# Nine products for twelve: sharing the q convolution's differences in both directions

## The chip, the cores and the metric

The kernel runs on one core of a Trainium2 chip. The metric is the device time of one execution in microseconds; lower is better. One execution of the kernel was also recorded by the profiler, and all views below come from that one.

## The reference

The input is a batch of 8 images with 256 channels of 64 x 64. Two layers follow each other. Layer 0 is an attention whose keys and values come from a 4 x 4 strided convolution of the image; its result is added to the image. Layer 1 is a linear attention at two scales:

```
qkv = einsum('oc,bchw->bohw', w_qkv, x)                # 768 channels
dw  = conv(qkv, w_dw, 5x5, padding 2, one filter per channel)
agg = einsum('goi,bgihw->bgohw', w_pw, dw in groups of 8)
ms  = concatenate([qkv, agg])                          # 64 heads, each 8 channels of q, k and v
q, k = relu(q), relu(k);  kv = k^T [v, 1];  out = q kv[:-1] / (q kv[-1] + 1e-15)
return x + batchnorm(w_proj out)
```

The change concerns the branch `agg`, and in it the q third: the depthwise 5 x 5 filter and the mixing of 8 channels into 8, together one convolution of 8 channels by 8 in each of 32 groups, followed by relu.

## The kernel before

The work goes in three passes over the batch, all in float32.

The **first pass** does layer 0 and the product with `w_qkv`, and writes q and k to HBM as *planes*: an image is cut into 16 phases (position within 4 x 4 cells), the 128 partitions hold 16 phases of a group of 8 channels, and the free dimension holds the cells, 17 x 17 with their border. On the side the generator `conv_weights` multiplies the depthwise and the mixing weights into the convolution's matrices and writes them to HBM (`wtd[j]`; j of 0 and 1 is q, 2 and 3 is k). A step of it runs once per step of the main loop, from step 17 on.

The **second pass** (`second_pass`) goes over 64 units `(t, k, b)`: half, block of four groups, image; the image runs fastest, so weights serve eight units. For a unit it convolves k (`what = 1`), forms the sums over positions of k with v at both scales (`summed_raw`, `summed`), and convolves q two units later (`what = 0`, for `q = u - 2`). A product maps the 128 values of a group's cell (16 phases by 8 channels) to the 128 values of an output cell; an output cell needs four of them, from the 2 x 2 input cells around it, so a square of 2 x 2 output cells would take 16. The kernel before shares products across only: for each pair of columns, `paired` (L1189 and L1190) makes the differences d0 - d1 and d2 - d1, and `convolve` computes three products instead of four, each for two rows `da` that are summed in PSUM, which makes 12 per square. A product with 128 columns covers a unit's 16 rows by 8 pairs of columns, so there are 3 x 2 x 4 groups = 24 of them per unit and convolution, recorded as 48 matmuls, since a float32 product appears as two records; L1248 issues those of k, L1252 those of q. The part with `i == 2` is common to both columns: ScalarE copies it from PSUM to the tile `both` (L1255), VectorE adds it to the other two (L1264), and ScalarE rectifies the sums into `r` (L1266 for k, L1268 for q).

All DMAs are issued by queue SP, in one order. For a unit these are: the tokens `kq` and `vq` of the next unit (L1165, L1177), the cells `d` of k and of q (L1158), the previous results `kv` and `kvg` (L1330, L1340), four stores of `r` to `qd` (L1347), and one of the four pieces of the next block's weights (L1152). Each of q's and k's weights has two buffers, used by turns, and so have the q cells. The framework places instructions on each queue by its own estimate, roughly in the order of the program, except for those marked `keep_in_program_order`.

The **third pass** divides and projects. Its first loads and products are called from the last units of the second (`next(ahead)`).

Of the kernel before, what the change touches and what calls it, by code (L numbers as in the profile page):

```python
# [27 lines left out]
F32 = mybir.dt.float32  # L28
# [546 lines left out]
def first_pass(ctx: ExitStack, tc: tile.TileContext, a, fine, planes, x2d, kd, vd, wtd):  # L575
# [98 lines left out]
    def conv_weights():  # L674
        for j in (2, 3, 0, 1):
            wd = made.tile([P, 16, 6, 16], F32, tag="wd", name=f"wd_{j}", bufs=1)
            nc.sync.dma_start(wd[:, :, :4], a.w_big[:, j].rearrange("p g (n f) -> p g n f", n=4))

            tc.keep_in_program_order(nc.vector.tensor_add(wd[:, :, 4:], wd[:, :, 0:4:2], wd[:, :, 1:4:2]))
            for g in range(16):  # L680
                w = made.tile([P, 6 * 16, D1], F32, tag="wb", name=f"wb_{j}_{g}", bufs=1)
                tc.keep_in_program_order(
                    nc.vector.tensor_tensor(
                        w,
                        wd[:, g].rearrange("p n f -> p (n f)").unsqueeze(2).to_broadcast([P, 6 * 16, D1]),
                        consts["wsmall"][:, j, g].unsqueeze(1).to_broadcast([P, 6 * 16, D1]),
                        ALU.mult,
                    )
                )
                nc.sync.dma_start(wtd[j][:, g], w.rearrange("p n o -> p (n o)"))  # L690
                yield
# [427 lines left out]

@with_exitstack  # L1120
def second_pass(ctx: ExitStack, tc: tile.TileContext, a, planes, kd, vd, wtd, kvd, kvg, qd, ahead):
    nc = tc.nc
    B = a.x.shape[0]
    def pool(name, bufs=1):
        return ctx.enter_context(tc.tile_pool(name=name, bufs=bufs))
# [3 lines left out]
    late, first, odd, const, second, small, mid, w_taps, pairs, sides, between, third, third_w, w_q, more = (  # L1129
        pool("late2", 2), pool("first2"), pool("odd2"), pool("const2"), pool("second2"), pool("small2", 2),  # L1130
        pool("mid2"), pool("taps2"), pool("pairs2", 2), pool("sides2", 2), pool("between2", 2), pool("third2"),
        pool("third_w2"), pool("wq2"), pool("more2"),
# [11 lines left out]
    wt, grids, cells, kqs, vqs = {}, {}, {}, {}, {}  # L1144


    def load_weights(u, what, g):
        t, k, b = units[u]
        if g == 0:
            home = (second if k % 2 else first) if what else (third_w if k % 2 else w_q)  # L1150
            wt[t, k, what] = home.tile([P, 4, 6 * P], F32, tag=f"w{what}_{k % 2}", name=f"w{what}_{t}_{k}")
        nc.sync.dma_start(wt[t, k, what][:, g], wtd[2 * what + t][:, 4 * k + g])  # L1152

    def load_cells(u, what):
        t, k, b = units[u]
        home = (odd if u % 2 else first) if what else (more if u % 2 else third)
        d = home.tile([P, 4, (NB + 1) ** 2], F32, tag=f"d{what}_{u % 2}", name=f"d{what}_{u}")
        nc.sync.dma_start(d, planes[b, 2 * what + t][4 * k : 4 * k + 4].rearrange("g p e -> p g e"))  # L1158
        grids[u, what] = d.rearrange("p g (y x) -> p g y x", x=NB + 1)
# [24 lines left out]
    def paired(u, what):  # L1184
        d = grids[u, what]
        c = (pairs if what else late).tile([P, 2 + what, 4, (NB + 1) * NB // 2], F32, tag=f"c{what}", name=f"c{what}_{u}")
        v = c.rearrange("p n g (y x) -> p n g y x", x=NB // 2)
        d0, d1, d2 = (d[:, :, :, i : i + NB - 1 : 2] for i in range(3))
        nc.vector.tensor_sub(v[:, 0], d0, d1)  # L1189
        nc.vector.tensor_sub(v[:, 1], d2, d1)  # L1190
        if what:

            nc.gpsimd.tensor_copy(v[:, 2], d1)
        cells[u, what] = c

    for g in range(4):
        load_weights(0, 1, g)
    load_cells(0, 1)
    load_tokens(0)
    load_cells(1, 1)  # L1200
# [8 lines left out]
    def load_taps(t):  # L1209
        taps.append((more if t else w_taps).tile([P, 4, 36, D1], F32, tag="taps", name=f"taps_{t}"))  # L1210
        nc.sync.dma_start(taps[t], a.w_taps[:, 4 * t : 4 * t + 4])
# [3 lines left out]
    load_cells(0, 0)  # L1215
# [3 lines left out]
    kts, reds, raws, mraws, state, qs, maggs = {}, {}, {}, {}, {}, {}, {}  # L1219
# [16 lines left out]
    def convolve(u, what, i):  # L1236
        t, k, b = units[u]
        c, w, d = cells[u, what], wt[t, k, what], grids[u, what]
        ps = bank("cv", f"cv{what}_{u}_{i}", 5)
        for g in range(4):  # L1240
            for da in range(2):
                n = 2 * da + i if i < 2 else 4 + da
                cols = slice(da * (NB // 2), da * (NB // 2) + P)
                x = d[:, g, da : da + NB, 1:NB:2] if i == 2 and not what else c[:, i, g, cols]
                m = w[:, g, n * P : (n + 1) * P]
                out = ps[:, g * P : (g + 1) * P]
                if what:
                    nc.tensor.matmul(out, x, m, start=(da == 0), stop=(da == 1))  # L1248
                else:
                    if i == 2:  # L1250
                        out = out.rearrange("p (y x) -> p y x", y=NB)
                    nc.tensor.matmul(out, m, x, start=(da == 0), stop=(da == 1))  # L1252
        if i == 2:
            both = between.tile([P, QB], F32, tag=f"both{what}", name=f"both{what}_{u}")
            nc.scalar.copy(both, ps)  # L1255

            home = (second if u % 2 else sides) if what else late
            r = home.tile([P, 2, 4, P], F32, tag=f"r{what}", name=f"r{what}_{u}", bufs=2 - what)
            state[u, what] = (r, both)
            (kts if what else qs)[u] = r  # L1260
        else:
            r, both = state[u, what]
            s = sides.tile([P, QB], F32, tag="s", name=f"s{what}_{u}_{i}")
            nc.vector.tensor_add(s, ps, both)  # L1264
            if what:
                nc.scalar.activation(r[:, i].rearrange("p h n -> p (h n)"), s, AF.Relu)  # L1266
            else:
                nc.scalar.activation(  # L1268
                    r.rearrange("p a h n -> p (a h n)").rearrange("p (h n two) -> p two h n", h=4, two=2)[:, i],
                    s.rearrange("p (h n) -> p h n", h=4),  # L1270
                    AF.Relu,
                )
# [69 lines left out]
    def stored(u):  # L1342
        t, k, b = units[u]
        r = qs.pop(u).rearrange("p a h n -> p (a h n)").rearrange("p (h n) -> p h n", h=4)
        for h in range(4):
            c0 = P * t + D0 * k + D1 * h
            put = nc.sync.dma_start(qd[b][c0 : c0 + D1].rearrange("d f n -> f d n"), r[:, h])  # L1347

            if u < n_all - 3:
                tc.keep_in_program_order(put)  # L1350

    positive(0)
    paired(0, 1)
    for u in range(n_all + 3):
        p, q, r = u - 1, u - 2, u - 3
        now, was, conv, out = u < n_all, 0 <= p < n_all, 0 <= q < n_all, 0 <= r < n_all
        if u == n_all - 5:
            next(ahead)
        if 0 < u < n_all:
            summed_raw(u)  # L1360
        if 1 < u < n_all - 1:
            load_tokens(u + 1)
        if 0 < p < n_all:
            load_cells(p, 0)
        if was:
            stored_raw(p)
        if conv:
            stored_agg(q)
        if out:
            stored(r)  # L1370
        if u == n_all - 3:
            next(ahead)
        if was:
            summed(p)
        if now:
            convolve(u, 1, 2)
        if u + 1 < n_all:
            paired(u + 1, 1)
        if now:
            convolve(u, 1, 0)  # L1380
            if u == 0:
                summed_raw(u)
            ended_raw(u)
            convolve(u, 1, 1)
        if u + 2 < n_all:
            load_cells(u + 2, 1)
        if u == 0:
            load_tokens(2)
            for g in range(4):
                load_weights(0, 0, g)  # L1390
            load_taps(1)
        if was:
            ended(p)
        if conv:
            paired(q, 0)
        if u == n_all - 1:
            next(ahead)
        if u == n_all:
            next(ahead)
        if u == n_all + 1:  # L1400
            ahead.send(lambda name: bank("cv", name, 5))
        if conv:
            convolve(q, 0, 2)
            convolve(q, 0, 0)

        if u + 1 < n_all:
            positive(u + 1)
        if conv:
            convolve(q, 0, 1)
        if now and u + B < n_all:  # L1410
            b = units[u][2]
            load_weights(u + B - b, 1 if b < 4 else 0, b % 4)
# [307 lines left out]
def kernel_body(ctx: ExitStack, tc: tile.TileContext, a, out):  # L1720
# [6 lines left out]
    def scratch(name, shape):  # L1727
        return dram.tile(shape, F32, tag=name, name=name)
# [13 lines left out]
    wtd = [scratch(f"wt_{j}", [P, 16, 6 * P]) for j in range(4)]  # L1742
# [131 lines left out]
```

## Time and profile before

| | |
|---|---|
| time, median of 3 runs | 3715.17 us (3711.45 to 3718.46) |
| profiled execution | 3715.08 us, span 3713.3 us |
| TensorE busy | 3653.4 us, 98% of the span |
| second pass, 1975 to 3066 us | PE busy 1072.6 of 1091 us, DMA share 0.90, 254 GB/s |
| q convolution, L1252 | 2048 + 1024 matmul records |
| k convolution, L1248 | 3072 matmul records |
| HBM read and written | 415.15 and 274.40 MB |

Rows of instruction groups give the busy time in microseconds and the mean duration of one instruction in nanoseconds. Matmuls overlap, so a row's mean is longer than the distance from one to the next. The chain of waits goes back from the last instruction of the program through whatever released each step; in its listing in order of time each piece has a start, a length and what it was. "DMA x<-y" in it is time until a transfer landed or could be queued. The slices are 40 equal parts of the span, about 93 us each.

### The profile page before, as it was taken

How to read it: one execution, taken by the hardware profiler on the slowest of the kernel's cores; microseconds unless marked ns; L12 is line 12 of the kernel's file. 1: busy time of each engine (PE TensorE's matmuls, PEld its weight loads, DVE VectorE, ACT ScalarE, POOL GpSimd, SP SyncE). 2: the span in 40 equal slices, each digit the busy share in tenths (PEclk: the TensorE clock that was granted, in tenths of full speed). 3: DMA queues.
4: the chain of work that ended last, by engine and by line, in shares of the span. 5: the costliest groups of instructions: out<-in, count | busy, mean ns of one | idle time of the engine just before them, and what ended most of it. 6: DMA issues, size and time to landing. Idle time of an engine off the chain costs nothing.

```text
span 3713.3 us, 65717 instructions
## 1 busy us (share of the span) xinstructions
PE 3653.4 (98%) x25506; PEld 2021.5 (54%) x25506; DVE 2051.1 (55%) x3159; ACT 1349.4 (36%) x2761; POOL 1366.2 (37%) x1394
## 2 busy tenths in 40 slices
PE   8999999999999999999998999999999999999998
PEld 4443534435334344353336888888888884433333
DVE  1567576675766755746675544444444445444442
ACT  3344354443443434434451222222222323333322
POOL 2334343343443433434442333334343321222222
PEclk9999999999999999999999999999999998999999
DMA  5336456464464553543648999889989868778773
GB/s 180 105 102 194 125 145 179 129 192 143 123 206 119 148 156 106 147 126 97 174 111 218 275 270 286 251 249 265 259 250 259 239 193 237 224 224 230 220 219 102
DMA packets 593936, 694.00 MB, mean 187 GB/s; under 512 B 84048, under 2 KB 453200, under 8 KB 593616
## 3 DMA queue, kind: packets, MB, share of 16 engines
q1 hardware_dynamic: 593616, 689.72, 65.6%
q8 instruction: 203, 3.33, 0.4%
q14 instruction: 117, 0.96, 0.1%
HBM read 415.15 MB, written 274.40 MB: 186 GB/s over the span
## 4 chain that ended last, share of the span: by engine, by line
PE 93%; DMA 3%; DVE 1%; ACT 1%; issue 1%; SPq 0%; POOL 0%; POOLq 0%; ACTq 0%; DVEq 0%
PE qkv L917 16%; PE p L1597 12%; PE cv L1248 9%; PE cv L1252 9%; PE sc L795 7%; PE sums L1298 7%; PE av L819 6%; PE o L873 6%; PE q L780 6%; PE sr L707 6%; PE den L839 3%; PE rep L1583 2%; PE den L1564 1%; PE raw L1281 1%; DMA vq<-v 1%; DMA d<-planes 1%
## 5 line engine op out<-in xcount | busy, mean ns | idle before, releaser
L832 POOL TENSOR_TENSOR ej<-e,e 128x512 f32<-128x512 f32 x512 | 679.4, 1356 | 958.2 <-ACT e L801 958.2
L801 ACT ACTIVATE e<-sc 128x512 f32<-128x512 f32 x1024 | 530.1, 607 | 581.7 <-PE sc L795 581.7
L1264 DVE TENSOR_TENSOR s<-cv,both 128x512 f32<-128x512 f32 x256 | 176.5, 690 | 384.5 <-PE cv L1248 197.0
L1248 PE MATMUL cv<-w,c 128*128 128x128 f32 x3072 | 378.2, 280 | 6.7 <-DVE eps L1619 6.2
L1248 PEld LDWEIGHTS cv<-w,c 128*128 128x128 f32 x3072 | 356.1, 193 | 36.4 <-issue 33.5
L1607 POOL TENSOR_TENSOR y<-z,xs 128x512 f32<-128x512 f32 x128 | 166.1, 1306 | 457.0 <-ACT z L1605 445.1
L1298 PE MATMUL sums<-vq,r 128*32 128x288 f32 x4096 | 307.3, 412 | 0.0
L795 PE MATMUL sc<-q,kk 32*128 32x512 f32 x2048 | 299.6, 639 | 0.0
L917 PE MATMUL qkv<-differences,combined 128*128 128x512 f32 x576 | 291.3, 597 | 0.5 <-POOL differences L890 0.4
L1597 PE MATMUL p<-raw,wp 128*128 128x512 f32 x512 | 246.9, 604 | 5.6 <-ACT z L1605 5.6
L819 PE MATMUL av<-e,vv 128*32 128x512 f32 x2048 | 248.4, 598 | 0.6 <-ACT e L801 0.6
L707 PE MATMUL sr<-x,wsr 128*128 128x256 f32 x1024 | 234.0, 382 | 8.0 <-DMA wsr<-in_w_sr_dram 7.5
L780 PE MATMUL q<-x,wq 128*128 128x512 f32 x512 | 241.9, 594 | 0.0
L1597 PE MATMUL p<-agg,wp 128*128 128x512 f32 x512 | 240.4, 592 | 0.0
L1252 PE MATMUL cv<-c,w 128*128 128x128 f32 x2048 | 239.0, 275 | 0.0
L1252 PEld LDWEIGHTS cv<-c,w 128*128 128x128 f32 x2048 | 234.3, 192 | 0.0
L873 PE MATMUL o<-att,wout 128*128 128x512 f32 x512 | 231.2, 593 | 0.0
L707 PEld LDWEIGHTS sr<-x,wsr 128*128 128x128 f32 x1024 | 194.8, 191 | 62.5 <-issue 30.7
L1255 ACT COPY both<-cv 128x512 f32<-128x512 f32 x128 | 75.0, 586 | 423.0 <-PE cv L1248 363.7
L852 DVE STREAM_TRANSPOSE rden<-den 128x512 f32<-128x512 f32 x128 | 90.9, 710 | 217.0 <-PE den L839 212.0
L788 ACT COPY q<-q 128x512 f32<-128x512 f32 x128 | 75.1, 587 | 372.0 <-PE q L780 372.0
L933 DVE TENSOR_TENSOR whole<-part,qkv 128x512 f32<-128x512 f32 x256 | 172.5, 684 | 67.7 <-ACT part L979 47.9
(143 smaller groups left out, 5280.6 us busy)
## 6 DMA issues: line engine op xcount, KB each, us to landing
planes<-stage SPq DMA_DIRECT2D x128, 578.0 KB
d<-planes SPq DMA_DIRECT2D x128, 578.0 KB
vq<-v SPq DMA_DIRECT2D x256, 256.0 KB
raw<-planes SPq DMA_DIRECT2D x64, 578.0 KB
x<-in_xp_dram SPq DMA_DIRECT2D x64, 512.0 KB
wsr<-in_w_sr_dram SPq DMA_DIRECT2D x128, 256.0 KB
x<-x SPq DMA_DIRECT2D x128, 256.0 KB
k<-turned SPq DMA_DIRECT2D x256, 128.0 KB
```

The costliest lines, as they stand in the source:

```text
L707: nc.tensor.matmul(ps[:, oc], w[:, ci, oc * P : (oc + 1) * P], strips(b, f // 2)[:, ci, f % 2 * NK : (f % 2 + 1) * NK], start=(f == ci == ...
L780: nc.tensor.matmul(ps, consts["wq"][:, ci, c * P : (c + 1) * P], strips(b, s)[:, ci], start=(ci == 0), stop=(ci == 1),)
L795: nc.tensor.matmul(scs[h], kks[b][rows, c, kc * P : (kc + 1) * P], qs[rows], start=True, stop=True)
L801: nc.scalar.activation(e, scs[h], AF.Exp, scale=D0**-0.5)
L819: nc.tensor.matmul(sums["av"][cols], vvs[b][:, kc, c * P + h * D0 : c * P + (h + 1) * D0], es[h], start=(kc == 0), stop=(kc == 1),)
L832: nc.gpsimd.tensor_tensor(e, es0[h], es1[h], ALU.add)
L873: nc.tensor.matmul(ps, consts["wout"][:, c, oc * P : (oc + 1) * P], att[c], start=(c == 0), stop=(c == 1))
L917: nc.tensor.matmul(ps, w, x, start=True, stop=True)
L1248: nc.tensor.matmul(out, x, m, start=(da == 0), stop=(da == 1))
L1252: nc.tensor.matmul(out, m, x, start=(da == 0), stop=(da == 1))
L1298: nc.tensor.matmul(ps[h * D0 : (h + 1) * D0, : 36 * D1].rearrange("p (r n e) -> p r n e", r=3, e=D1), kt[:, par, h, 2 * r + c], vq[:, r : ...
L1597: nc.tensor.matmul(as_block(ps, i // 2), wp[:, i, oc * P : (oc + 1) * P], block(g, i // 2, i % 2, j), start=(i == 0), stop=(i == 3),)
```

## The change

The q convolution now shares in both directions. For a square of 2 x 2 cells, the 3 x 3 input cells around it are combined to nine inputs: differences across (`across`, columns 0 and 2 minus the middle column), and of these and of the middle column differences down (`down`, on VectorE and GpSimd). Nine weight combinations, prepared in the first pass, multiply them, one product each and none summed in PSUM; `product` adds the results: the middle one is copied to `both`, two `side` sums and four `part` sums are built from it, and four last additions complete the four cells. Two images are done together, 64 squares each, so a product again has 128 columns. The nine products of a pair are spread over two units: four in the even, five in the odd one.

```diff
 def conv_weights():
+    for j, half in ((j, half) for j in (2, 3, 0, 1) for half in range(2)):
+        n = 6 if j > 1 else 9
+        wd = made.tile([P, 8, n, 16], ...)         # was [P, 16, 6, 16], four loads in all
+        nc.sync.dma_start(wd[:, :, :4], ...)
+        yield
+        ... 4:6 = 0:4:2 + 1:4:2
+        if n == 9:
+            ... 6:8 = 0:2 + 2:4;  8 = 4 + 5
         # per group: w = wd * wsmall, n * 128 values (were 768 for all), then its store
+        # for n == 9 the store is laid out "n p o -> p n o", runs of 512 bytes
```
```diff
+Q_ORDER = ((1, 1), (0, 1), (2, 1), (1, 0), (0, 0), (2, 0), (1, 2), (0, 2), (2, 2))
+
+    def load_weights_q(u, which):
+        home = w_q.tile([P, len(which), 4, P], F32, tag=f"w0_{len(which)}", ...)
+        for i, ij in enumerate(which):
+            nc.sync.dma_start(home[:, i], wtd[t][Q_WEIGHTS[ij], :, 4 * k : 4 * k + 4])
+
+    def load_cells_q(m):
+        d = third.tile([P, 4, 2, (NB + 1) ** 2], F32, tag="d0", ...)       # one buffer, two images
+        for i in range(2):
+            nc.sync.dma_start(d[:, :, i], planes[b, t][4 * k : 4 * k + 4]...)
+
+    def across(m, j):
+        nc.vector.tensor_sub(c, d[:, :, j : j + NB - 1 : 2], d[:, :, 1:NB:2])     # 1088 values
+
+    def down(m, j):
+        nc.vector.tensor_sub(v[:, 0], c0, c1)                                      # 512 values
+        nc.gpsimd.tensor_tensor(v[:, 1], c2, c1, ALU.subtract)
+
+    def product(m, i, j):
+        for g in range(4):
+            x = column(m, j)[:, g, :, 1:NB:2] if i == 1 else y_j[:, i // 2, g]
+            nc.tensor.matmul(out, w[:, g], x, start=True, stop=True)
+        (1, 1): now.both = copy of ps (ScalarE)
+        (0, 1), (2, 1): side_i = ps + both
+        (1, 0), (1, 2): part_0 = ps + side_0;  part_2 = ps + side_2
+        the other four: part_i += ps, then relu into now.r (ScalarE)
```
```diff
 for u in range(n_all + 3):
-        if 0 < p < n_all: load_cells(p, 0)
+        if u % 2 and u < n_all: load_cells_q(u // 2)
-        if out: stored(r)                                # 4 stores, each unit
+        if u % 2 == 0 and u > 2: stored(u // 2 - 2)      # 8 stores, each second unit
+        if conv and u % 2 == 0: across(q // 2, 0); down(q // 2, 1)
         ... convolve(u, 2)
+        if conv and u % 2: down(q // 2, 2)
+        products(u, 0)
         ... convolve(u, 0)
+        if conv and u % 2 == 0: down(q // 2, 0); across(q // 2, 2)
+        products(u, 1)
         ... convolve(u, 1)
+        if u == 0: load_weights_q(0, Q_ORDER[:4]); load_weights_q(0, Q_ORDER[4:])
+        if was and p == n_all // 2 - 1: load_taps(1)     # was at u == 0, in a buffer of its own
+        products(u, 2)
-        convolve(q, 0, 2), convolve(q, 0, 0), convolve(q, 0, 1)
-        if now and u + B < n_all: load_weights(u + B - b, 1 if b < 4 else 0, b % 4)
+        if now and u + B < n_all and 2 <= units[u][2] < 6: load_weights(u + B - b, b - 2)
+        if conv and units[q][2] >= B - 2 and u < n_all:
+            load_weights_q(u - u % 2, Q_ORDER[4:] if u % 2 else Q_ORDER[:4])
```

The q weights have one buffer, in a part of four blocks and a part of five, in place of two buffers. The q cells (`d0`) and the results (`r0`) have one buffer each, for two images. `both` is one tag with two buffers for k and q.

## The prediction

> **What bounds the kernel now.** I read the page's busy shares first, then the forty slices, then a table by stretches of the second pass.
>
> ```profile
> PE 3653.4 (98%) x25506; PEld 2021.5 (54%) x25506; DVE 2051.1 (55%) x3159; ACT 1349.4 (36%) x2761; POOL 1366.2 (37%) x1394
> PE   8999999999999999999998999999999999999998
> DMA  5336456464464553543648999889989868778773
> ```
>
> TensorE is busy everywhere, so removed matmuls should count almost in full, unless something close behind takes over. The DMA row says what: from slice 21 (about 1,975 us) to slice 32 (about 3,066 us), which is the second pass, it stands at 8 and 9 where the first pass shows 3 to 6.
>
> ```profile
> 2050.00:2300.00 250.00, 248.17 (x3402) 215.35 (x3404) 118.60 (x228) 71.01 (x105) 96.80 (x106) 1.00 1.00 278
> 2300.00:2900.00 600.00, 600.00 (x8240) 519.97 (x8233) 290.78 (x544) 171.69 (x252) 240.13 (x252) 1.00 0.89 254
> ```
>
> These are the stretch and its length, then busy us of PE, PEld, DVE, ACT and POOL, the clock, the DMA share and GB/s. From 2,300 us on PE never idles and DMA keeps a tenth in hand. Before that DMA is full at 278 GB/s while it works off what had piled up at the start, and PE already loses a little. The chain of waits shows both states:
>
> ```profile
> 2116.12 3.77 PE cv L1248 x32
> 2125.40 9.42 DMA vq<-v
> 2134.91 5.92 DMA d<-planes
> 2143.90 9.48 DMA vq<-v
> ...
> 2406.82 5.64 PE cv L1252 x48
> 2423.42 5.64 PE cv L1252 x48
> ```
>
> In the first state transfers lie on the chain; in the second only PE does, one unit per 16.60 us. A unit's q convolution is the 48 matmul records on L1252 (24 products, two records each), 5.64 us, so 0.1176 us per record. Queue SP tells the states apart as well, by how long it needs for the same eight token loads:
>
> ```profile
> 2125.40 9.23 SPq L1177 DMA_DIRECT2D vq<-v  x8
> ```
> ```profile
> 2401.36 5.64 SPq L1177 DMA_DIRECT2D vq<-v  x8
> ```
>
> **What the Trainium skill says.** "Perfetto Trace Analysis", section "Identifying the Most-Contended Engine", warns that matmul busy time overstates nearness to the limit and that the DMA share misleads too, bytes per second being the measure. The trace agrees: PEld is 520 of 600 us where PE shows 600, and full DMA shares go with 267 to 298 GB/s over 50 us. "SBUF — State Buffer", section "Who interferes with whom", says that a DVE instruction with two SBUF inputs contends with a GpSimd one that reads SBUF; here the subtraction on L1189 has a median of 0.72 us and a maximum of 1.89. "TensorE: Matmul & The Clock Gate", section "HAM oscillation", says that PE gaps over some 3.4 us slow its clock; the clock is 0.90 in 1,950 to 2,000 us, where PE idles most.
>
> **The change, part by part.**
>
> *Matmuls.* q now takes 3,072 records (64 units by 48). After: 32 pairs by 9 products by 4 groups by 2 records = 2,304. The 768 that go, at 0.1176 us, are 90.3 us, all on PE's path: 1.41 us per unit, 16.60 to 15.19. The moving operand of three products in nine is read in runs of eight values. The nearest row is the old L1252 form on d, mean 290 ns beside 275; if each of 32 x 3 x 8 = 768 records loses half of that, 6 us come back; at best none. I take none.
>
> *DMA bytes.* By the page's issue sizes a unit moves kq 512, vq 1,536, d 2 x 578, q 4 x 128, small stores 21 and weights 384 KB, together 4.22 MB. The cells and the stores of q keep bytes and packet sizes. q weights become nine blocks of 256 KB per eight units where four of 384 KB were: +96 KB per unit, 4.32 MB. A unit of 15.19 us would need 284 GB/s. In the full state SP needed 203.67 us for 13 units (its stores of kvg at 2,042.81 and 2,246.48 us), 15.67 us each at 272 GB/s; with 98 thousand bytes more, 16.0. The best 100 us anywhere in the second pass moved 285 GB/s (summed from the trace's packet records), so 15.2. **DMA thus bounds the new unit at 15.2 to 16.0 us**, at or above PE's 15.19; I take 15.9, near the measured full state.
>
> *Bursts.* The weight loads were one per unit. They become w1 in units 2 to 5 of each eight, and four and five q blocks in units 0 and 1: 4.9 and 5.1 MB there, 17.8 and 18.8 us at 272 GB/s, and 3.8 MB in units 6 and 7. Each q load waits for the last product that reads its half of the buffer (two buffers alternated before); behind it on SP stand the next unit's stores, tokens and cells. The new weights are wanted two units later, so what suffers is the tokens behind them, with some 7 us in hand. Not carried over from one unit to the next, the bursts add up to 0.2 us per unit; zero if carried. My 15.9 holds part of that.
>
> *The start.* The first d0 and the second taps (1.17 MB) leave the opening loads, q weights grow there from 1.57 to 2.36 MB, wanted two units later: 0, under the token loads that PE waits for anyway.
>
> *Other buffers with one copy.* Both images' q cells (d0, 1.18 MB) load from the start of an odd unit and are wanted some 7 us into the next even one, about 23 us; r0's eight stores (1.05 MB) have about as long before ScalarE writes the next pair's first result into that buffer. At 272 GB/s each needs 4 us once it is its turn. Late cells stop PE at a product; late stores stop ScalarE, and behind it on its queue stand the copies of both, which free PE's banks, and the rectifying of the next keys. Taken at 0 here, priced under the rivals. The two `both` buffers are now shared by k and q: three copies per pair rotate through them, each free within half a unit, 0. The second taps load (576 KB) moves to unit 32, where only one DVE product of the next unit wants it: 0 to 3 us, once; I take 0.
>
> *DVE, ACT, POOL.* Per pair, four c subtractions (0.72) and four additions (0.69), 5.64 us, become two subtractions of 1,088 values (no row; the rows of 288, 512 and 768 values, 457, 690 and 949 ns, give about 1.28), three of 512 (0.69) and ten additions (0.69), 11.5 us. DVE goes from 8.0 to 11.0 us per unit, POOL from 6.6 to 8.7 (three of 1.36 us per pair), ACT falls by 0.3. All lie beside PE. Five banks, each filled in 0.94 us, cover a DVE delay of some 4 us; without that cover PE would wait for evacuations. Bounds 0 to 0.3 us per unit; I take 0.
>
> *First pass.* DVE's weight products: 32 grow from 949 to about 1,343 ns, +12.6 us; additions go from 4 x 0.69 to about 6.3 us, +3.5. The waits of DVE for wd (6.1 us, three times) go, a step now standing between load and addition. SP issues four loads more and 6.3 MB more are stored in 512-byte runs, at a DMA share of 0.53. From 300 to 1,300 us PE is busy 997 of 1,000 us and DVE 667: it hides there; 0 to 3 us, I take 1.
>
> *Sum.* 64 x (16.6 - 15.9) = 45 us saved, 1 lost: -44. The profiled execution took 3,715.08 us (span 3,713.3), as good as the median of 3,715.17, so both bases give 3,671; I say 3,670. On PE alone it would be 3,625.
>
> **Rivals.** *PE stays the bound.* For it: the packet records give 285 GB/s over the best 100 us and 300 over 33. Against: full shares held 272 to 274 for 200 us. With 15.2 to 15.4 us per unit, 3,625 to 3,640. Chance 0.25.
>
> *Nothing is left.* SP still waits for r before its stores (80.9 us in 700), now for eight at once; if that idle time adds to the full state, 16.0 becomes 16.5 and the time 3,708 to 3,722. Chance 0.07.
>
> *Slower: d0 is late.* The place is the first q product of each even unit, which reads d0 directly. Behind stores, tokens and, in weight units, q blocks, SP has to move up to 5.6 MB (20.6 us at 272 GB/s) in those 23 us. If PE waits over 2.8 us per pair, what two units save is gone; at 4 us it is 32 x 1.2 = 38 us slower, 3,753, and waits that long also cost clock. For it: d waits are already DVE's longest on DMA. Against: only one pair in four carries weights. Chance 0.10.
>
> *DMA takes over*, as forecast: 3,650 to 3,700, chance 0.58.
>
> **The numbers.** A measurement here tells 0.2% from no change, 7.4 us. The forecast and the first rival give faster, 0.83; same 0.07; slower 0.10. The range runs from the PE bound to the no-change case, 3,625 to 3,710.
>
> **What would show it.** Right: L1252's successor with 2,304 records; DMA at 0.97 or more and 270 to 285 GB/s through the whole second pass; chain pieces of vq, d or w after 2,300 us; PE visibly below full there. Wrong: PE at 100% at 284 GB/s or more (first rival); PE waiting for DVE or ACT instead; one long d0 wait in each even unit.

## The result, and the profile after

| | median, us | ratio to before, 95% interval |
|---|---|---|
| before, measured beside it | 3717.06 (3708.97 to 3723.0) | |
| after | 3701.66 (3693.05 to 3706.44) | 0.9957 [0.9942, 0.9972] |

The change makes the kernel faster by 15 us, where 45 were forecast. The profiled execution of after took 3693.05 us (span 3691.2), the fastest of its seven, so its views show a little less than what is typically lost. In the views PE is TensorE and PEld its weight loads, DVE is VectorE, ACT ScalarE, POOL GpSimd and SP the queue that issues the transfers. The page has the 768 matmul records fewer:

```profile
PE 3574.2 (97%) x24738; PEld 1926.9 (52%) x24738; DVE 2316.4 (63%) x3395; ACT 1328.1 (36%) x2729; POOL 1563.9 (42%) x1490
...
PE   8999999999999999999998999999999999999998
...
DMA  5336446465474663543647999999999988777773
```

DMA is now at 9 through the second pass. The same two stretches as before (length; busy us of PE, PEld, DVE, ACT, POOL; clock, DMA share, GB/s) say that it is nevertheless not full:

```profile
2050.00:2300.00 250.00, 241.50 (x3308) 202.77 (x3306) 186.61 (x289) 68.62 (x101) 149.78 (x132) 0.99 0.94 268
2300.00:2900.00 600.00, 565.10 (x7906) 467.72 (x7908) 435.34 (x675) 162.63 (x238) 351.30 (x311) 0.99 0.93 265
```

PE idles 35 us of 600 and DMA stops at 0.93 and 265 GB/s, where before had held 278 over 250 us. Neither is full: something makes each wait for the other. From one product `p` on DVE (L1394) to the next, a unit takes 16.43 us on average, against 16.60 before and 15.19 on PE alone, and the units alternate between 13.6 and 19.4 us. In the profiled executions the second pass begins 2.8 us earlier (1,982.78 before, 1,979.96 after), the first product of the third pass comes 23.2 us earlier (3,093.0 and 3,069.8): nearly all of the 22 us that these two executions differ by lies in the second pass, and so does what is missing.

The chain of waits of after, in one of the long units (start, length, what):

```profile
2614.25 6.56 DMA vq<-v
2620.83 8.16 DMA d<-planes
...
2629.11 0.06 DVE c L1233
...
2630.32 0.68 DVE s L1314
...
2636.81 1.04 ACT kq L1285
...
2637.90 1.08 PE raw L1367 x64
2638.98 2.62 PE sums L1384 x22
```

This is the key reading. L1233 is `across`, the new subtraction on the q cells. The program writes it in the even unit, where the cells are wanted. DVE's own order (start, duration, instruction, in brackets the idle time before it) shows it earlier:

```profile
2624.53 0.69 DVE L1357 TENSOR_TENSOR part<-part,cv 128x512 f32<-128x512 f32 x1 [0.20 <-PE cv L1329]
2629.11 1.29 DVE L1233 TENSOR_TENSOR c<-d 128x1088 f32<-128x1088 f32 x1 [3.89 <-DMA d<-planes]
2630.32 0.68 DVE L1314 TENSOR_TENSOR s<-cv,both 128x512 f32<-128x512 f32 x1
2630.92 0.18 DVE L1410 COPY mraw<-raw 128x32 f32<-128x32 f32 x1
2631.02 0.15 DVE L1411 COPY mraw<-raw 128x1 f32<-128x1 f32 x1
2631.09 1.28 DVE L1354 TENSOR_TENSOR side<-cv,side 128x512 f32<-128x512 f32 x2
```

The framework put `across` of the next pair into the odd unit, ahead of that unit's own additions (L1314 for k, L1354 and L1357 for the pair still at work). SP has only just requested the cells (at 2,619.91, behind eight token loads), so DVE stands 3.89 us, with finished PSUM banks behind it. What they hold up is in the waits from 2,300 to 2,900 us (engine and line, what it waited for: total us, times, longest):

```profile
DVE c L1233 <- DMA d<-planes: 42.3, 17, 5.3
...
PE sums L1384 <- ACT r L1315: 20.6, 14, 2.9
...
PE raw L1367 <- ACT kq L1285: 12.8, 15, 1.1
```

The last two lines are 33.4 of PE's 35 us. PE's sums need k rectified (L1315), which needs the addition that is queued behind `across`; ACT's next keys (L1285) stand behind that again. (The 51 us in the expectation of e1_pin below add PEld's 30.7 us for the same waits to PE's 20.6.)

A second thing shows on queue SP: eight stores in a row where there were four, before the next tokens can be asked for. The row gives start and duration of all eight, 0.76 us each:

```profile
2606.24 6.06 SPq L1434 DMA_DIRECT2D q<-r  x8
```

### The profile page after: what moved, and what is told of

Same layout as the page of the kernel before. It is cut to its first block, busy times and chain, and to the rows that moved or that the text cites. A ratio compares the mean times of both kernels' runs of the same rounds, so it can differ in the third digit from the quotient of the medians.

```text
span 3691.2 us, 64550 instructions
## 1 busy us (share of the span) xinstructions
PE 3574.2 (97%) x24738; PEld 1926.9 (52%) x24738; DVE 2316.4 (63%) x3395; ACT 1328.1 (36%) x2729; POOL 1563.9 (42%) x1490
## 4 chain that ended last, share of the span: by engine, by line
PE 74%; DMA 17%; SPq 3%; DVE 3%; issue 2%; ACT 1%; POOL 0%; POOLq 0%; DVEq 0%; ACTq 0%
PE qkv L929 16%; PE p L1699 12%; DMA vq<-v 8%; PE sc L807 7%; PE av L831 6%; PE o L885 6%; PE q L792 6%; PE sr L719 6%; DMA d<-planes 5%; PE cv L1298 3%; PE den L851 3%; PE cv L1329 2%; PE rep L1685 2%; PE sums L1384 2%; SPq L1434 2%
## 5 line engine op out<-in xcount | busy, mean ns | idle before, releaser
L1384 PE MATMUL sums<-vq,r 128*32 128x288 f32 x4096 | 317.9, 420 | 29.4 <-ACT r L1315 27.1
L1384 PEld LDWEIGHTS sums<-vq,r 128*32 128x32 f32 x4096 | 146.0, 112 | 141.5 <-ACT r L1315 42.1
L1329 PE MATMUL cv<-y,w 128*128 128x128 f32 x1536 | 204.1, 279 | 3.4 <-DVE y L1248 2.1
L929 PE MATMUL qkv<-x,wqkv 128*128 128x512 f32 x384 | 188.8, 611 | 5.2 <-ACT e L813 5.2
L1329 PEld LDWEIGHTS cv<-y,w 128*128 128x128 f32 x1536 | 185.9, 193 | 5.0 <-issue 4.9
```

The lines of the kernel that those rows point to most:

```text
L929: nc.tensor.matmul(ps, w, x, start=True, stop=True)
L1329: nc.tensor.matmul(out, w[:, g], x, start=True, stop=True)
L1384: nc.tensor.matmul(ps[h * D0 : (h + 1) * D0, : 36 * D1].rearrange("p (r n e) -> p r n e", r=3, e=D1), kt[:, par, h, 2 * r + c], vq[:, r : ...
```

## The experiments

They ran against the kernel before, whose median was between 3713.1 and 3716.8 us beside them. The theory: the change's own costs are (1) where `across` stands on DVE and (2) the eight stores on SP. The rivals: the 96 KB per unit of q weights, their bursts, DVE's added work, d0's single buffer. The names say where a run starts from: b runs from the kernel before, e runs from the change.

**What the matmuls and the bytes are worth alone.** b1 takes the kernel before and leaves out six of 24 q products, so 768 records; b2 adds the bytes.

```diff
 # b1: before, convolve() for q
+                    if da == 1 and (i == 2 or (i == 0 and g < 2)):
+                        continue
 # b2: b1, and in each unit that loads a piece of q weights
+                nc.sync.dma_start(more_w, wtd[t2][:, 4 * k2 + b % 4, : 3 * P])    # 192 KB
```

> The kernel before with 6 of its 24 q products per unit left out (the second row of i = 2, and two groups of i = 0), that is 768 records fewer, as many as the change takes away, and nothing else touched: DMAs, DVE, ACT and POOL as before. It prices the matmuls alone. PE bound: 90 us less, 3,625. Bandwidth theory as forecast (15.5 to 15.7 us per unit with the old bytes): 3,655 to 3,675. If it stays within 20 us of before, the old order of transfers already allowed no shorter unit, and the new buffers and the new placement cost nothing.

> The kernel before with 18 products (b1, 3,648 us) and one more load of 196 KB in every second unit, 96 KB per unit: the bytes that the change adds and nothing else of it (the loaded block is read by nobody; six of 24 q products per unit are left out as in b1). If the second pass is bound by bytes at b1's 274 GB/s: +0.36 us per unit, 64 units, +23 us: 3,671. If bytes are not what holds the change back: within 5 us of b1, 3,643 to 3,653.

b1: 3647.99 us, 0.9814 [0.9798, 0.9831]. b2: 3670.57, 0.9872 [0.9851, 0.9892]. The stretch of b1 and of b2, columns as above:

```profile
2300.00:2900.00 600.00, 584.35 (x8222) 496.94 (x8221) 297.03 (x576) 176.44 (x267) 243.06 (x267) 0.99 0.98 274
```
```profile
2300.00:2900.00 600.00, 582.80 (x8108) 483.11 (x8108) 276.49 (x567) 175.03 (x264) 226.47 (x262) 1.00 0.98 274
```

In both the DMA share is 0.98 at 274 GB/s while PE is not full, and 96 KB more per unit cost 22.6 us or 0.35 us per unit, as worked out: with this order of transfers on SP the bytes set the time (b8 below shows that another order moves the same bytes faster). What the forecast described is b2, and b2 took what was forecast, 3,670. So the change loses 31 us to something that b2 does not have.

**across in its written order.** e1_pin keeps the order that the program has for `across` and `down`:

```diff
-        nc.vector.tensor_sub(c, d[...j...], d[...])
+        tc.keep_in_program_order(nc.vector.tensor_sub(c, d[...j...], d[...]))     # down's two likewise
```

> The changed kernel with the instructions of across and down kept in program order on VectorE and GpSimd, so that the subtraction that waits for the q cells d0 no longer stands ahead of the odd unit's additions; same DMAs, same products. Placement theory (the late d0 costs because DVE waits for it with the k and q additions behind it, and through ScalarE's r and kq the sums of PE): the waits of PE's sums for r, 51 us in 600, go, units of 16.4 us become 15.6 to 15.9, the time 3,665 to 3,680, and the DMA rate rises to 272 to 280 GB/s. Bandwidth theory (268 GB/s is all that the DMA engines give this mix, whoever waits): the same idle time turns up elsewhere, as DMA waits of PE or DVE, and the time stays at 3,695 to 3,707.

3688.04 us, 0.9927 [0.9914, 0.994]: some 13 us of the 31. The units become even (16.2 and 16.3 us), PE's waits for L1315 go, and `across` waits 1.8 us once in the same 600 us. SP's own waits for the single buffer of the q weights (L1177) fall from 15.2 us in after to 0.9. The run pins `down` too, on DVE and on GpSimd; that the cost lay on DVE is told by the waits of PE in after, of which none names GpSimd. But DMA stays at 0.94:

```profile
2300.00:2900.00 600.00, 575.60 (x7977) 485.51 (x7976) 436.11 (x683) 164.08 (x240) 342.88 (x315) 0.98 0.94 268
```

**d0 earlier.** e3_both has e1_pin and asks for d0 in the even unit, as soon as its last reader in the program is past.

```diff
-        if u % 2 and u < n_all: load_cells_q(u // 2)
         ...
         products(u, 1)
+        if u % 2 == 0 and u < n_all: load_cells_q(u // 2)
```

> As e1_pin, and the two loads of d0 are put ahead of the next unit's cells and tokens on SP, where the previous pair's last reader of that buffer is through. Placement theory: d0 is no longer late anywhere, the time is that of e1_pin or up to 10 us less. Bandwidth theory: what is moved ahead of the tokens makes the tokens late instead; no better than the changed kernel, 3,695 to 3,710.

3741.39 us, 1.0076 [1.0064, 1.0088]: slower than before, which neither expectation had. DMA fell to 0.91 and 259 GB/s, and the waits (again 2,300 to 2,900 us) show PE stopped by `down`, and ACT by transfers:

```profile
ACT r L1335 <- DMA vq<-v: 54.5, 9, 9.5
...
PE cv L1329 <- DVE y L1248: 31.1, 13, 5.3
```

An earlier d0 in this place is thus no remedy. It puts 1.18 MB ahead of the next cells and tokens on SP, so these are asked for later; which of them did the harm was not taken apart.

**The q weights.** e4 loads them once and uses the first block's for all blocks; e6 does so in e1_pin; b3 gives b1 the change's bursts.

```diff
 # e4, e6
-        if conv and units[q][2] >= B - 2 and u < n_all:
-            load_weights_q(...)
 # b3: b1, q pieces two each in units 6 and 7, k pieces in units 2 to 5
```

> The changed kernel with the q weights loaded once and used for all blocks (left out: the seven later loads of nine blocks, so that the q results of later blocks are computed with the first block's weights). 288 KB per unit, 7% of the bytes, go; order and placement of all else stay. Bandwidth theory: the unit shortens by 295 thousand bytes at 268 GB/s, 1.1 us, to 15.3, the time falls by some 65 us to 3,635. Placement theory: d0 lands earlier only in the weight units, one pair in four; the time falls by 10 to 25 us, and PE's waits for r stay in the other pairs.

> The change with across and down kept in their written order (as e1_pin, 3,688) and with the q weights loaded once (as e4, 3,670; leaves out the seven later loads of the nine blocks). If the two costs add (13 and 31 us): 3,657. If they are one wait counted twice: 3,668 or more. If DVE's added work or d0's single buffer is a cost of its own that neither touches, the rest above b1's 3,648 is it: 3,657 would leave 9 us for these.

> b1 (six of 24 q products per unit left out) with the same bytes, but the q weights' four loads of 393 KB requested two each in units 6 and 7 of eight and the k weights' in units 2 to 5, as the change orders its own. If bursts cost nothing (the prediction): 3,648. If a burst makes two units of eight late by what it adds (2 x 393 KB at 274 GB/s less one load's worth, 1.4 us each, once or twice per eight units): 3,659 to 3,670.

e4: 3670.18 us, 0.9875 [0.986, 0.9889]. e6: 3638.17, 0.9792 [0.9777, 0.9806]. b3: 3649.25, 0.9823 [0.9807, 0.9838], the same as b1. So a burst of two q pieces per unit costs nothing. e6 is below what either theory gave:

```profile
2300.00:2900.00 600.00, 595.90 (x8457) 506.54 (x8459) 455.60 (x727) 179.25 (x260) 353.59 (x333) 1.00 0.95 268
```

With `across` in its place and 288 KB per unit less to load, PE is at 596 of 600 us, though DVE does all of its added work (456 us) and d0 has its one buffer. Neither is therefore a cost in itself. Nor does a saving add to e1_pin's as a sum: 13 and 31 us alone, 63 together.

**Cells and stores by twos, in b1.** b5 does both, b6 the stores only, b7 the cells only.

```diff
-        if 0 < p < n_all: load_cells(p, 0)
+        if u % 2 and u < n_all: load_cells(u - 1, 0); load_cells(u, 0)         # b5, b7
-        if out: stored(r)
+        if u % 2 == 0 and u > 2: stored(u - 4); stored(u - 3)                  # b5, b6
```

> b1 (six of 24 q products per unit left out) with q's cells (d0) and q's stores two images at a time in every second unit, as the change has them; bytes and weights as in b1. If taking them by twos costs nothing: 3,648. If d0 by twos is what is late (the change's DVE waits up to 5.3 us for it, PE 4.4 us per pair): 32 pairs at 1 to 2 us: 3,680 to 3,712, with DVE's c waiting for d at one unit of two and units that alternate.

> b1 (3,648 us; six of 24 q products per unit left out) with only q's stores by twos: eight stores in a row in every second unit, q's cells each unit as before. If the eight stores are the cost of b5 (31 us; SP issues them in some 5.6 us, 0.7 us per 128 KB or 187 GB/s, and the DMA engines run dry behind them): 3,670 to 3,682. If it is the cells: 3,648 to 3,653.

> b1 (six of 24 q products per unit left out) with only q's cells (d0) by twos, stores each unit as before. If the cells are the cost of b5 (a late d0 that DVE waits for): 3,670 to 3,682. If it is the stores: 3,648 to 3,653.

b5: 3679.42 us, 0.99 [0.9881, 0.9919]. b6: 3645.86, 0.9813 [0.98, 0.9827]. b7: 3678.32, 0.99 [0.9885, 0.9915]. This seemed to acquit the stores and convict the cells, but b7 holds a wait that the change does not have. Its SP waits for the matmuls (L1254) that still read the second image's buffer:

```profile
SPq L1158 <- PE cv L1254: 33.7, 11, 7.5
```

Everything behind that load on SP waits too; that is the 30 us, at least in part. In the change d0 is free by then. b5 and b7 thus say nothing of the change, and only b6 is kept: eight stores in a row cost nothing in that order of loads.

**Cells and stores in the change.** e7 puts the second image's four stores at the end of the even unit, e8 on ACT's queue.

```diff
 # e7, on e1_pin
-            stored(u // 2 - 2)
+            stored(u // 2 - 2, (0,))
 ...
+        if u % 2 == 0 and u > 2: stored(u // 2 - 2, (1,))       # last in the unit
 # e8, on e1_pin
-                put = nc.sync.dma_start(...)
+                put = (nc.scalar if i else nc.sync).dma_start(...)
```

> The change with across and down in their written order (e1_pin, 3,688) and the second image's four stores requested at the end of the unit, behind d1 and the weights, the first image's where they were. If a row of eight stores is what lets the DMA engines run dry: 3,665 to 3,680, DMA share above e1_pin's 0.94. If only the number of stores counts, or if d0 is the cause: 3,685 to 3,691.

> e1_pin (3,688) with the second image's four stores issued on ACT's queue, right behind the last relu of q on that engine, and not on SP's. If SP's issue of eight stores is what lets the DMA engines run dry: 3,662 to 3,675, DMA share 0.96 or more. If ACT's own relus for PE come late behind its four issues (2.8 us of ACT per pair): 3,690 to 3,720. If d0 is the cause and the stores are not: 3,685 to 3,691.

e7: 3669.06 us, 0.9883 [0.9868, 0.9898]. e8: 3656.94, 0.9832 [0.9811, 0.9853].

```profile
2300.00:2900.00 600.00, 589.12 (x8303) 499.69 (x8301) 457.62 (x719) 172.78 (x253) 351.56 (x329) 1.00 0.98 282
```

In e8 DMA is full at 282 GB/s and a unit takes 15.37 us. e7 has a share of 0.96 at 276 GB/s. So the stores' place on SP does cost in the change: against e1_pin, e7 gains 19 us with all stores still on SP, e8 31. How, is to be seen in part in e1_pin. Queue SP has this row of stores (start, duration),

```profile
2504.38 7.14 SPq L1434 DMA_DIRECT2D q<-r  x8
```

and the table by stretches, in slices of 2 us around it, reads:

```profile
2502.00:2504.00 2.00, 2.00 (x87) 1.30 (x82) 2.00 (x2) 1.26 (x2) 1.92 (x2) 1.00 1.05 273
2504.00:2506.00 2.00, 2.00 (x47) 1.15 (x34) 1.78 (x3) 0.00 (x0) 1.92 (x2) 1.00 0.83 212
2506.00:2508.00 2.00, 2.00 (x20) 2.00 (x18) 1.90 (x4) 0.33 (x1) 1.92 (x3) 1.00 0.59 149
2508.00:2510.00 2.00, 2.00 (x20) 2.00 (x19) 0.48 (x2) 0.84 (x2) 1.92 (x3) 1.00 0.60 167
2510.00:2512.00 2.00, 2.00 (x21) 2.00 (x20) 0.98 (x2) 0.00 (x0) 0.69 (x1) 1.00 0.45 117
```

Before the stores DMA is full (the last columns are its share and GB/s); while SP issues them, 128 KB each, it falls to half, because SP needs longer to issue a store than the engines to move it and the queue runs out. PE is busy in these slices and waits later. What it then waits for, from 2,300 to 2,900 us in e1_pin, shows a possible second path from the stores to PE:

```profile
POOL c L1224 <- DMA d<-planes: 179.7, 27, 10.5
...
PE raw L1408 <- POOL red_raw L1280: 12.1, 6, 3.7
```

L1224 is GpSimd's copy of k's cells (d1), which SP asks for right behind the eight stores. The reductions `red_raw`, which PE needs, stand behind that copy on GpSimd. It is the pattern of `across` once more, on another engine.

**What covers the stores.** In b6 a load of q cells (578 KB) stands ahead of the eight stores on SP (with only `kv` and `kvg` between), in the change the four smallest pieces of vq (128 KB each). e13 moves one line so that d1 stands there.

```diff
+        if u + 2 < n_all: load_cells(u + 2)      # was behind convolve(u, 1)
         if was: stored_raw(p)
```

> e1_pin (3,688) with the load of d1 (578 KB, 2.1 us of the DMA engines) requested ahead of the eight stores and not behind them; nothing else moved. If the bytes that stand queued when SP comes to the stores decide whether the DMA engines run dry: 3,665 to 3,680, DMA share above 0.95. If they do not: 3,685 to 3,691.

> e13 with the second image's four stores on ACT's queue (as e8, 3,657). If e8 had taken what there is: 3,652 to 3,660. If d1 earlier covers the four stores left on SP as well: down towards PE's own time, 3,640 to 3,650.

e14 has e8's line for the stores besides. e13: 3670.14 us, 0.9878 [0.9861, 0.9894]; e14: 3657.95, 0.9851 [0.983, 0.9872].

```profile
2300.00:2900.00 600.00, 584.16 (x8190) 492.30 (x8188) 442.94 (x699) 169.25 (x247) 346.41 (x323) 0.98 0.97 275
```

Moving one load ahead of ten small issues is worth 18 us. The idle share of the DMA engines, summed over slices of 1 us from 2,300 to 2,900 (in us), goes with it; in brackets the part in slices whose middle lies within a store on SP or 1.5 us after it:

| b1 | b6 | after | e1_pin | e13 | e8 |
|---|---|---|---|---|---|
| 38 (18) | 42 (33) | 69 (51) | 64 (51) | 44 (32) | 40 (15) |

From e1_pin to e13 nearly all of the idle time that goes lies at the stores, which speaks for the queue that runs out. But d1 also arrives earlier. In e13 the wait of GpSimd's copy is

```profile
POOL c L1224 <- DMA d<-planes: 77.1, 8, 12.7
```

and PE no longer waits for `red_raw`. e7 and e8 bring d1 forward too, since fewer stores stand ahead of it. That the row of stores costs is shown; how much of it comes through the idle engines and how much through the late d1 is not.

**Is it the number of issues?** b8 puts b1's stores on ACT's queue, e11 makes the nine q weight loads of e1_pin four of the same bytes.

```diff
 # b8, on b1
-                put = nc.sync.dma_start(...)
+                put = nc.scalar.dma_start(...)
 # e11, on e1_pin; blocks sorted by their place in wtd, n of them in one load
+        nc.sync.dma_start(home[:, :n], wtd[t][n0 : n0 + n, :, 4 * k : 4 * k + 4].rearrange("n p g o -> p n g o"))
+        nc.sync.dma_start(home[:, n], wtd[t][Q_WEIGHTS[which[n]], :, 4 * k : 4 * k + 4])
```

> b1 (3,648; six of 24 q products per unit left out) with all of q's stores on ACT's queue instead of SP's: the same bytes, four issues of some 19 per unit off SP. If SP's issues set the rate: down to what PE needs, 15.19 us per unit, 0.38 us less than b1's 15.57: 3,624. If the bytes set it: 3,645 to 3,650, DMA share still 0.98.

> e1_pin (3,688) with the nine q weight loads per eight units made four, of 768, 256, 1,024 and 256 KB: the same bytes, five issues fewer on SP's queue. If SP's issues set the rate (5 of 8 units x 0.7 us = 0.44 us per unit, 64 units): 3,660. If the bytes set it: 3,685 to 3,691.

b8: 3651.32 us, 0.9833 [0.9819, 0.9846]; e11: 3676.95, 0.9901 [0.9886, 0.9916]. As a whole b8 gains nothing, but its trace is not that of b1:

```profile
2050.00:2300.00 250.00, 237.11 (x3278) 199.00 (x3278) 115.66 (x239) 70.73 (x108) 95.45 (x107) 0.99 1.00 291
2300.00:2900.00 600.00, 597.35 (x8541) 509.95 (x8544) 312.22 (x589) 188.27 (x281) 260.33 (x278) 1.00 0.94 277
```

From 2,300 us on PE is full, and a unit takes 15.24 us where b1 takes 15.77, with the same loads and stores. So 0.98 and 274 GB/s in b1 were the limit of that order of issues, not of the engines for these bytes. What is won there is lost at both ends: the first ten units take 168 us where b1 takes 151, and from the last product `p` to the end of the program b8 needs 9 us more. Why was not taken apart. b8's total is thus near the expectation for a bound of bytes, while its steady stretch fits the other one, PE's own 15.19 us per unit.

The Trainium skill, "Perfetto Trace Analysis", section "What 'DMA-bound' means", names the issuing queue as a bound of its own, to be known by a track that is solid with DMA slices. In b1 SP's rows cover 725 of the 850 us from 2,050 to 2,900, 588 without the pauses inside the rows, and part of that is waiting for full engines, as the token loads of 5.64 and 9.23 us in the kernel before show. The track is not solid, and yet b8 shows that the queue held b1 back from 2,300 us on. "Trainium Kernel Development and Optimization", section "Key Constraints", says that issuing from several engines only saves the sequencer's issue time, all queues sharing the same 16 engines; the steady units of b8 agree with that. A part of e8's 31 us, perhaps the 12 by which it beats e7, may be of this kind and have nothing to do with the row of eight. e11 lies between the two expectations and settles nothing by itself.

**Both together, and the best version.** e9 is e8 without the written order of `across`; e10 is e8 with e11's loads.

```diff
 # e9: the change as it is, and e8's line for the stores
+                put = (nc.scalar if i else nc.sync).dma_start(...)
 # e10: e1_pin, this line, and e11's two loads
```

> The change as it is, with the second image's four stores on ACT's queue (e8 without the written order of across and down). If across's place on DVE costs its own 13 us whatever SP does: 3,670. If it costs only because d0 comes late behind SP's stores: 3,655 to 3,661.

> e8 (3,657) and e11 together: written order, second image's stores on ACT's queue, q weights in four loads. If SP's issues still bind after e8: 3,638 to 3,645, PE's own time (as e6). If the bytes bind by then (4.32 MB per unit at 282 GB/s is 15.3 us): 3,652 to 3,660.

e9: 3688.47 us, 0.9933 [0.992, 0.9947]. e10: 3652.03, 0.9831 [0.9817, 0.9844]. With e9 the four corners are known:

| us | `across` as placed | in written order |
|---|---|---|
| eight stores on SP | 3701.7 | 3688.0 |
| four of them on ACT | 3688.5 | 3656.9 |

Either repair brings 13 us alone and 31 on top of the other; the two waits lie partly on top of each other. In e9 `across` waits for d longer than in after, 86.0 us in the same stretch, so an earlier d0 by freer queues does not mend its place. e10 beats both kernels: 63 us under before, 50 under after, though not clearly under e8 and e14.

## Why the prediction was right and where it failed

- **Matmuls, 90.3 us.** Right: 2,304 records, and in e6, where PE is the bound, 77 us of it arrive.
- **DMA takes over, 15.9 us per unit.** Right as to what the added bytes cost: b2's 3,670.6 is the forecast, at 274 GB/s. The 272 GB/s taken from the full state are, however, the rate of SP's order and not of the engines: b8 moved the bytes of b1 in 15.24 us per unit where b1 took 15.77. It named 0.97 or more and 270 to 285 GB/s as what would show it; after had 0.93 and 265. In e8, with the waits gone, it was 0.98 and 282, near the best 100 us (285) that the trace of before had shown, and 15.37 us per unit, in the lower part of the range 15.2 to 16.0.
- **Bursts, 0 to 0.2.** b3's cost nothing; those of the change, of four and five loads, were not tried apart. (By its own bytes and rate the two units take 17.9 and 18.9 us, not 17.8 and 18.8; nothing rests on it.)
- **Cells and stores of two images, taken at 0.** This is one step that failed. It gave the eight stores 4 us "once it is its turn" and asked only who waits for r0. The runs show that SP issues the stores for 5 to 7 us, in which the DMA share falls to between 0.45 and 0.83 in the row shown, and that the cells of k behind them come late at GpSimd. Measured on e1_pin, moving the stores or the load behind them was worth 18 to 31 us. The rival "nothing is left" had the eight stores at once adding idle time to the full state, at 3,708 or more, with a chance of 0.07; that was the right kind of loss, with the wrong reason (SP's wait for r, which is 4.3 us in 600 in after).
- **DVE, taken at 0, bounds 0 to 0.3 us per unit.** This is the other. Its busy time did no harm (e6), though it was 11.9 us per unit by the stretch of after where 11.0 were forecast: `across` took 1.58 us in the mean and the `down` of its results 1.25, where 1.28 and 0.69 had been reckoned; why was not tested. The cover named, five PSUM banks, was not what mattered: PE waited for rectified k and keys, two engines behind one subtraction that waited for a load. That cost 13 us with all stores on SP and 31 with half of them on ACT's queue, 0.2 to 0.5 us per unit. "PE waiting for DVE or ACT instead" stood among the signs that would make the forecast wrong, and it came.
- **Slower: d0 is late.** The cells were late, but at DVE in the odd unit, not at PE's first product in the even one. The place named is where the program has the first reader; the framework, which orders by its own estimate, had put a reader earlier.
- **Start, taps, strided operand, first pass.** Of the strided products, those that read d have a median of 297 ns and those that read c 275, like the others; e6 leaves at most 13 us above PE's 3,625 for all of these together.

## What to carry to other kernels

When a change turns steady loads and stores into rows of twice the length every second step, look at the transfer queue's issue times beside the bytes, and at which load stands behind the row: one large load moved from behind it to ahead of it was worth 18 us. When an instruction with a DMA for its input is added to an in-order engine, find out where the scheduler really puts it, and ask what stands behind it; its own microseconds can be free and its place dear. A run whose total does not move can still have changed its bound, as b8 did, so compare stretches and not totals alone. And a forecast from busy time and bytes is that of the kernel with neither wait: build that kernel, here by leaving work out of the old one, to tell the bound from the waits.

## What the runs showed of the hardware

A 128 KB store took SP 0.52 us to issue at the least and 0.60 in the median (152 stores in e1_pin from 2,300 to 2,900 us), which with the 0.04 us between two of them is some 205 GB/s, below the 274 to 282 that the DMA engines hold over 600 us in b1 and e8. In such a row the pace of issues therefore sets the rate. A DMA share of 0.98 did not mean that the bytes needed the time: b1 had it at 274 GB/s and 15.77 us per unit, and with its stores on ACT's queue (b8) the same units took 15.24 us at a share of 0.94.
